# A written-out head for an attention and density kernel: statistics, weights, projections and maxima ahead of the loop

## The chip, the cores and the metric

The kernel runs on one core of one Trainium2 chip. The metric is the device time of one execution in microseconds. The profile is one execution on the same chip, with the start and end of every instruction.

## The reference, cut to what matters

The input is x of 8 images, 192 channels, 64 x 64 pixels (N = 4096 pixels per image), in fp32. Layer 0 is an attention over the pixels of an image with a residual, layer 1 a density model per channel with a residual.

```python
# layer 0: gn is a group norm over 32 groups of 6 channels
q = prelu(conv1x1(gn(x), w1, b1), a1)            # 24 channels
k = prelu(conv1x1(gn(x), w2, b2), a2)            # 24 channels
v = prelu(conv1x1(gn(x), wa, ba), aa)            # 192 channels
score = softmax(einsum('bnc,bcm->bnm', q, k), axis=2)
x = x + einsum('bnm,bmc->bnc', score, v)
# layer 1: per channel a chain 1 -> 3 -> 3 -> 3 -> 1, at gn(x) - 0.5 and gn(x) + 0.5
logits = einsum('cij,cjn->cin', softplus(ms[i]), logits) + bs[i]
logits = logits + tanh(fs[i]) * tanh(logits)      # after the first three layers
x = x + maximum(abs(sigmoid(sign * upper) - sigmoid(sign * lower)), 1e-6)
```

## The kernel before

A tile holds 64 groups of three channels twice: partitions 0 to 63 are the first half of the pixels, 64 to 127 the second half. Eight pieces `d` of an image (`NP`), each 256 pixels of both halves, are the unit of the projections; two loads of 192 KB bring one. Pieces of image 0 wait in the buffers `d3` to `d10` of the density's pool (`xi["first", 0, d]`).

**The loop** (from L1258) runs over 8 x 128 = 1024 steps `t`. A step has the score products of step t + 1 (`scores`, L701, with an exponential on ScalarE, L705), the products and the reduce of a row maximum `LEAD` = 22 steps ahead (`max_step`, L644 and L648), and the attention product of step t (`attend`, L716: 16 matmul instructions). The projections, statistics and maxima of the next image, and the density of the image before, are put between the steps by a planner. It keeps a table of due times (`at`, `due`) and a list of jobs (`job`, `start_job`) that need room in PSUM: of the two accumulators `turns` (b0, b1) the one that attention does not use in these 16 steps is the guests' place (`misc`), and `guest` says from when each of its two banks is free. A job has a rank and the number of banks that it takes. What is written in the program's order stays in that order on each engine: there is no other scheduler. PSUM holds four pairs of banks: b0, b1, `sc` and `mx`.

**The head** is what stands before the loop, and it is where the change is. In order of the program:

- 16 loads of image 0 on SP's queue (L103).
- `ident`, and on VectorE `gavg`, the matrix that averages over groups.
- On ScalarE's queue the slopes (L152), eight loads of biases (L170, L171, which wait for VectorE's memsets of `bq` and the reduce into `bk`), eight loads of weights (L181 to L184) and 22 small loads of the density's parameters (L215).
- VectorE copies the weights into the layout of the matmuls (L187 to L198) and works out the density's parameters (L230 to L274: softplus of `mm`, products of the first two linear layers, and so on), with one Exp and one Tanh on ScalarE (L231, L246).
- Statistics of image 0 (`norm_stat`, L378: 16 instructions), aggregation and the group's mean and variance over TensorE (`norm_end`, L387 to L426), weights times the scale (`weights`, L469 to L501).
- `settle` runs the planner until it has nothing to do: `keys` of all eight pieces and `queries` of the first two (L544, L573), each followed by two ScalarE evacuations with Relu (L529) into one of two scratch pairs `pra`, `prb`, and one VectorE instruction that makes PReLU of them (L532).
- `values` (L601), two jobs per piece, are handed to the planner, and 22 calls of `max_step` follow, one planner step each. All projections go through the same guests' place, all maxima through `mx`. When sixteen maxima are there, `max_end` transposes them (L668) and adds them to q (L673).

A maximum of one chunk covers 128 rows of scores and 1024 columns: two matmuls that contract over 24 rows, each in a row group of 32, then one reduce. Chunk `k` uses the row groups 0 and 1 where `k` is even, 2 and 3 where it is odd.

Of the kernel before, what the change touches and what calls it, by code (L numbers as in the profile page):

```python
# [9 lines left out]
F32 = mybir.dt.float32  # L10
AF = mybir.ActivationFunctionType
# [6 lines left out]
def kernel(  # L18
# [131 lines left out]
    slope = const.tile([128, 3], F32, name="slope")  # L150
    for i, a in enumerate((a1, a2, aa)):
        nc.scalar.dma_start(out=slope[:, i : i + 1], in_=a.partition_broadcast(128))  # L152
    nslope = const.tile([128, 3], F32, name="nslope")
    nc.vector.tensor_scalar(nslope, slope, -1.0, None, ALU.mult)

# [7 lines left out]
    for t in (w1r, w2r, bq, ba_row, one_row):  # L163
        nc.vector.memset(t, 0.0)
# [4 lines left out]
    for k in range(4):  # L169
        nc.scalar.dma_start(out=bq[32 * k : 32 * k + CR, 0:1], in_=b1.unsqueeze(1))  # L170
        nc.scalar.dma_start(out=bk[32 * k : 32 * k + CR, 0:1], in_=b2.unsqueeze(1))  # L171
    for t in (bq, bk):
        nc.vector.tensor_scalar(t[:, 1:2], t[:, 0:1], -1.0, None, ALU.mult)
# [11 lines left out]
    for k in range(4):  # L185
        at = slice(32 * k, 32 * k + CR)
        nc.vector.tensor_copy(w1r[:, :, at], s1)  # L187

        p = slice(R * (k % 2), R * (k % 2) + R)
        nc.vector.tensor_copy(w2r[p, :, at], s2[p])  # L190
    for g in range(3):
        nc.vector.tensor_copy(
            wa_sb[:, g, :].rearrange("p (h r) -> p h r", h=3),
            sa[:, g, :].rearrange("p (r h) -> p h r", h=3),
        )
    for s in range(2):
        p = slice(R * s, R * s + 1)
        nc.vector.tensor_copy(  # L198
            ba_row[p].rearrange("p (h r) -> p h r", h=3),
            sb[p].rearrange("p (r h) -> p h r", h=3),  # L200
        )
# [7 lines left out]
    for src, dst, at, n in (  # L209
# [4 lines left out]
        for s in range(2):  # L214
            nc.scalar.dma_start(  # L215
                out=dst[R * s : R * s + R, :, at : at + n],
                in_=src.rearrange("(r g) i j -> r g (i j)", g=3),
            )


# [7 lines left out]
    sp = bufs[1][:, 0:432].rearrange("p (a g n) -> p a g n", a=6, g=3)  # L228
    e = sp[:, 0]
    nc.vector.scalar_tensor_tensor(e, mm, -1.0, mm, ALU.mult, ALU.max)  # L230
    nc.scalar.activation(e, e, AF.Exp, scale=-1.0)  # L231
    d = sp[:, 1]
    nc.vector.tensor_scalar(d, e, 2.0, None, ALU.add)
    nc.vector.reciprocal(d, d)
    s = sp[:, 2]
    nc.vector.tensor_tensor(s, e, d, ALU.mult)
    z = sp[:, 3]
    nc.vector.tensor_tensor(z, s, s, ALU.mult)
    p = sp[:, 4]
    nc.vector.tensor_scalar(p, z, 1.0 / 15.0, None, ALU.mult)  # L240
    for k in (13.0, 11.0, 9.0, 7.0, 5.0, 3.0):
        nc.vector.scalar_tensor_tensor(p, p, 1.0 / k, z, ALU.add, ALU.mult)
    nc.vector.scalar_tensor_tensor(p, p, 1.0, s, ALU.add, ALU.mult)
    nc.vector.tensor_scalar(d, mm, 0.0, None, ALU.max)
    nc.vector.scalar_tensor_tensor(wsp, p, 2.0, d, ALU.mult, ALU.add)
    nc.scalar.activation(tf, ff, AF.Tanh)  # L246
    q = sp[:, 5, :, 0:3]
    nc.vector.tensor_copy(lb, cb[:, :, 3:6])
    for j in range(3):
        w1j = wsp[:, :, 3 + j : 12 : 3]  # L250
        nc.vector.tensor_tensor(
            lc[:, :, j::3], w1j, tf[:, :, j : j + 1].to_broadcast([128, 3, 3]), ALU.mult
        )
        nc.vector.tensor_tensor(
            q, w1j, cb[:, :, j : j + 1].to_broadcast([128, 3, 3]), ALU.mult
        )
        nc.vector.tensor_tensor(lb, lb, q, ALU.add)
        dst = q if j else la
        nc.vector.tensor_tensor(
            dst, w1j, wsp[:, :, j : j + 1].to_broadcast([128, 3, 3]), ALU.mult  # L260
        )
        if j:
            nc.vector.tensor_tensor(la, la, q, ALU.add)

# [3 lines left out]
    nc.vector.tensor_copy(wx[:, :, 0, :], wsp[:, :, 0:3])  # L268
    nc.vector.tensor_copy(wx[:, :, 1, :], la)
    for i, k in enumerate((-0.5, 0.5)):  # L270
        nc.vector.scalar_tensor_tensor(
            bx[:, i, :, 0, :], wsp[:, :, 0:3], k, cb[:, :, 0:3], ALU.mult, ALU.add
        )
        nc.vector.scalar_tensor_tensor(bx[:, i, :, 1, :], la, k, lb, ALU.mult, ALU.add)  # L274
# [12 lines left out]
    guest = [0, 0]  # L287
# [10 lines left out]
    def misc():  # L298
        return turns[(now[0] // STEPS + 1) % 2]
# [10 lines left out]
    def start_job(t):  # L310
        p = t % STEPS
        for n, (rank, make, hold, banks, cols) in enumerate(jobs):
            if stream[0] and (p < 3 or p + max(hold, 1) >= STEPS):
                continue
            at_ = [i for i in range(2) if guest[i] <= t]
            if len(at_) < banks:
                if rank < 2:
                    return
                continue
# [4 lines left out]
            pm = misc()  # L324
# [302 lines left out]
    def max_step(m):  # L627
        b, n, i = m // IMG, m % IMG // STEPS, m % STEPS
        if b >= B:
            return  # L630
        if i == 0:
            rowmax[b, n] = small.tile([128, 4, 4], F32, tag="rm", bufs=3, name=f"rm_{b}_{n}")
# [18 lines left out]
        if i == STEPS - 1:  # L651
            max_end(b, n)
# [662 lines left out]
```

## Time and profile before

| what | us |
|---|---|
| median of 3 runs | 5038.0 (5033.52 to 5038.48) |
| the profiled execution, its own time | 5034.38 |
| its span, first to last instruction | 5032.6 |
| TensorE busy in the span | 4804.2 (95%) |
| VectorE busy | 4306.7 (86%) |
| ScalarE busy | 3204.3 (64%) |
| GpSimd busy | 510.7 (10%) |
| first attention product starts at | 167.10 |

The profile's lines name a kernel line (L716), the engine, the operation and its tiles (written <- read). A number behind x is a count of instructions; an fp32 matmul makes two in the records. In brackets stands the idle time before and what ended it. PE is TensorE, PEld its weight loads, DVE VectorE, ACT ScalarE, POOL GpSimd; SPq and ACTq are the queues on which these engines issue DMAs. PEclk is the share of its full clock that TensorE was granted. Times count from the first instruction. Idle time of an engine that others don't wait for costs nothing.

### The profile page before, as it was taken

The numbers are of one execution on the slowest core, as the hardware profiler recorded it, in microseconds if no ns is written. First come the engines' busy times: TensorE is split into PE (matmuls) and PEld (weight loads), VectorE is DVE, ScalarE is ACT, GpSimd is POOL, SyncE is SP. The second block draws the span as 40 slices with busy tenths as digits, with TensorE's granted clock in tenths as the row PEclk, the third lists the DMA queues.
The fourth block names the chain that finished last, engine by engine and source line by source line (L and its number), as shares of the span: only waits on it lengthen the run. The fifth ranks groups of instructions, "written<-read, shape, count | busy, mean of one in ns | idle before, by whom it ended". The sixth has DMA issues, their size and how long they took to land.

```text
span 5032.6 us, 69853 instructions
## 1 busy us (share of the span) xinstructions
PE 4804.2 (95%) x29152; PEld 3531.2 (70%) x29152; DVE 4306.7 (86%) x4455; ACT 3204.3 (64%) x3710; POOL 510.7 (10%) x493
## 2 busy tenths in 40 slices
PE   4999999999999999999999999999999999999596
PEld 2677777777777777777777777777777777777342
DVE  3433338999899998999899998999899998999878
ACT  1233336777677766777677766677677776677765
POOL 0000000111111200120101110120111110120000
PEclk9999999999999999999999999999999999999798
DMA  2000011010111112001111112001110111000000
GB/s 54 26 16 10 20 28 30 21 37 24 35 30 30 28 34 46 18 22 39 33 33 28 27 34 49 18 18 41 37 33 22 33 27 25 11 10 17 9 9 17
DMA packets 111952, 135.48 MB, mean 27 GB/s; under 512 B 14738, under 2 KB 93076, under 8 KB 111636
## 3 DMA queue, kind: packets, MB, share of 16 engines
q1 hardware_dynamic: 105856, 130.58, 10.6%
q8 instruction: 228, 3.74, 0.3%
q10 hardware_dynamic: 5780, 0.44, 0.1%
q14 instruction: 88, 0.72, 0.1%
HBM read 105.82 MB, written 25.17 MB: 26 GB/s over the span
## 4 chain that ended last, share of the span: by engine, by line
PE 72%; DVE 23%; ACT 3%; issue 1%; DMA 1%; POOL 1%; ACTq 0%; POOLq 0%; DVEq 0%
PE b L716 42%; PE sc L701 16%; DVE d L958 15%; DVE rm L648 5%; PE b L601 3%; PE b L899 2%; PE mx L644 2%; PE b L573 2%; PE b L544 1%; PE sc_tail L899 1%; PE mx_tail L899 1%; DVE st L378 1%; PE b L749 1%; ACT d L951 1%; PE b L668 1%
## 5 line engine op out<-in xcount | busy, mean ns | idle before, releaser
L716 PEld LDWEIGHTS b<-v,e 128*128 128x128 f32 x16384 | 2660.0, 190 | 779.1 <-issue 779.1
L716 PE MATMUL b<-v,e 128*128 128x193 f32 x16384 | 2963.8, 335 | 0.0
L705 ACT ACTIVATE e<-sc 128x1024 f32<-128x1024 f32 x1024 | 1046.2, 1022 | 1412.9 <-PE mx L644 1349.0
L648 DVE TENSOR_REDUCE rm<-mx 128x1 f32<-128x1024 f32 x1024 | 1248.8, 1220 | 556.5 <-PE mx L644 552.3
L644 PE MATMUL mx<-k,q 24*128 24x512 f32 x4096 | 1164.5, 645 | 23.4 <-DVE rm L648 23.1
L701 PE MATMUL sc<-q,k 25*128 25x512 f32 x4096 | 1158.1, 642 | 4.2 <-ACT e L705 4.0
L958 DVE SCALAR_TENSOR_TENSOR d<-d,wsp,d 128x1024 f32<-128x1024 f32 x768 | 985.6, 1284 | 47.3 <-ACT d L951 35.2
L958 DVE SCALAR_TENSOR_TENSOR d<-d,lc,d 128x1024 f32<-128x1024 f32 x765 | 968.3, 1279 | 16.3 <-ACT d L935 3.3
L958 DVE SCALAR_TENSOR_TENSOR d<-d,tf,d 128x1024 f32<-128x1024 f32 x543 | 681.4, 1280 | 4.0 <-ACT d L941 3.9
L941 ACT ACTIVATE d<-d 128x1024 f32<-128x1024 f32 x543 | 570.1, 1055 | 72.2 <-DVE d L958 71.3
L701 PEld LDWEIGHTS sc<-q,k 25*128 25x128 f32 x4096 | 307.2, 183 | 237.3 <-issue 201.2
L1040 POOL MEMSET pause<- 128x1 f32 x240 | 23.7, 99 | 4079.3 <-DVE d L958 4079.3
L951 ACT ACTIVATE d<-d,cb,wsp 128x1024 f32<-128x1024 f32 x351 | 433.1, 1235 | 7.1 <-DVE d L958 5.6
L926 ACT ACTIVATE d<-xc,bn,wn 128x1024 f32<-128x1024 f32 x288 | 353.3, 1233 | 4.5 <-DVE bn L438 4.4
L644 PEld LDWEIGHTS mx<-k,q 24*128 24x128 f32 x4096 | 309.1, 184 | 64.5 <-DVE rm L648 60.2
L935 ACT ACTIVATE d<-xc,bn,wn 128x1024 f32<-128x1024 f32 x255 | 314.5, 1234 | 0.1
L1087 POOL TENSOR_TENSOR d<-d,d 128x512 f32<-128x512 f32 x80 | 168.2, 2102 | 0.1
L1075 POOL TENSOR_TENSOR d<-d,d 128x512 f32<-128x512 f32 x80 | 166.3, 2078 | 7.8 <-DVE d L958 7.1
L1095 POOL TENSOR_TENSOR d<-d,d 128x512 f32<-128x512 f32 x80 | 159.6, 1995 | 2.1 <-POOL pause L1040 0.3
L601 PE MATMUL b<-wv,xi 64*128 64x192 f32 x1344 | 139.5, 340 | 0.0
L601 PEld LDWEIGHTS b<-wv,xi 64*128 64x128 f32 x1344 | 106.5, 186 | 25.4 <-issue 23.8
L1079 ACT ACTIVATE d<-d 128x512 f32<-128x512 f32 x160 | 91.8, 623 | 32.9 <-POOL d L1075 26.0
(157 smaller groups left out, 2337.3 us busy)
## 6 DMA issues: line engine op xcount, KB each, us to landing
xi<-in_x_dram SPq DMA_DIRECT2D x392, 192.0 KB, 3.5
xc<-in_x_dram SPq DMA_DIRECT2D x64, 384.0 KB, 5.8
out_dram<-xc SPq DMA_DIRECT2D x96, 256.0 KB, 3.1
d<-in_x_dram SPq DMA_DIRECT2D x16, 192.0 KB, 3.6
d<-in_wat_dram ACTq DMA_DIRECT2D x2, 144.0 KB
cb<-in_den_b_dram ACTq DMA_DIRECT2D x6, 2.2 KB
ff<-in_den_f_dram ACTq DMA_DIRECT2D x6, 2.2 KB, 4.8
bq<-in_b_dram ACTq DMA_DIRECT2D x4, 0.1 KB
```

The lines of the kernel that those rows point to most:

```text
L601: nc.tensor.matmul(pv[:, s, 0:C], lhsT=t[p, g, k * 128 : k * 128 + 128] if g < 3 else one_row[p], rhs=wf["v", b][p, g, :] if g < 3 else wf ...
L644: nc.tensor.matmul(sc[:, s, :], lhsT=tile_of(qt[b, n // 2], n, j)[r], rhs=kt[b][r, u : u + F], start=True, stop=True,)
L648: nc.vector.tensor_reduce(out=rowmax[b, n][:, j, k : k + 1], in_=sc, axis=AX.XY, op=ALU.max)
L701: nc.tensor.matmul(sc[:, s, :], lhsT=kt[b][r, k : k + 128], rhs=qt[b, n // 2][r, :, u : u + 256], start=True, stop=True,)
L705: return lambda: nc.scalar.activation(e, sc, AF.Exp)
L716: nc.tensor.matmul(a[:, j, 0 : C + 1], lhsT=e[:, s, j * 128 : j * 128 + 128], rhs=v[:, s, p % 4, :], start=p == 0 and s == 0 and j % 2 == ...
L899: nc.tensor.matmul(out[:, h, :], lhsT=diag[g][:, 3 * i + n - 1 if n else 9 + i, :], rhs=src[:, h * F : h * F + F], start=n == 0, stop=n == 3,)
L926: nc.scalar.activation(self.buf[k], self.src(), AF.Tanh, bias=bn[:, s, g, 0, i : i + 1], scale=wn[:, g, 0, i : i + 1],)
L935: nc.scalar.activation(self.buf[k], self.src(), AF.Identity, bias=bn[:, s, g, 1, i : i + 1], scale=wn[:, g, 1, i : i + 1],)
L941: nc.scalar.activation(self.buf[k], self.buf["l", k[1], k[2]], AF.Tanh)
L951: nc.scalar.activation(self.buf[k], self.buf["l", n - 1, 0], AF.Identity, bias=offset, scale=wsp[:, g, w : w + 1],)
L958: nc.vector.scalar_tensor_tensor(dst, src, factor, dst, ALU.mult, ALU.add)
```

## The change

The 16 statistics now stand ahead of everything else on VectorE but the first memsets; the copies of the weights go to GpSimd (`spread`), and the sign changes of biases and slopes stand behind the statistics (`negatives`). On ScalarE's queue the weights come first, then biases and slopes; the 22 parameter loads go to SP's queue, behind image 0.

The density's parameters become a generator, `parameters`, with the same 36 VectorE and two ScalarE instructions. The loop takes one of them per step from step 4 on, ahead of the step's scores and maxima.

The planner gets a list of rooms, `homes`, in place of `misc` and `guest`: a job goes to the room that has been free longest. In the head these are b0, b1 and the pairs `sc` and `mx`; in the loop there is one again, the accumulator that attention leaves free.

The head after the weights is written out: each planner step takes the next projection of a list (query 0, key 0, query 1, keys 1 to 7, then the sixteen values in attention's order), and from the ninth step on a pair of maxima, chunks `k` and `k + 1`, one into `sc` and one into `mx`: both products first, then both reduces. Eight such pairs make the sixteen maxima of the first block; key 6 and key 7 stand among the first of them, since chunks 0 and 1 need keys 0 to 3 alone. Six single maxima of the second block follow, each into `sc`. `max_step` is split into `place`, `max_products` and `max_reduce`; in the loop it does what it did. The line numbers of the changed kernel: statistics L407, aggregation L416, scaled weights L498, keys L573, queries L602, values L630, maxima L669 and L677, scores L738, attention L753.

```diff
-    slope = const.tile([128, 3], F32, name="slope")
-    for i, a in enumerate((a1, a2, aa)):
-        nc.scalar.dma_start(out=slope[:, i : i + 1], in_=a.partition_broadcast(128))
-    nslope = const.tile([128, 3], F32, name="nslope")
-    nc.vector.tensor_scalar(nslope, slope, -1.0, None, ALU.mult)
-
...
-    for t in (w1r, w2r, bq, ba_row, one_row):
+    slope = const.tile([128, 3], F32, name="slope")
+    nslope = const.tile([128, 3], F32, name="nslope")
+    for t in (bq, w1r, w2r, ba_row, one_row):
         nc.vector.memset(t, 0.0)
     nc.vector.memset(one_row[0:1], 1.0)
...
-    for k in range(4):
-        nc.scalar.dma_start(out=bq[32 * k : 32 * k + CR, 0:1], in_=b1.unsqueeze(1))
-        nc.scalar.dma_start(out=bk[32 * k : 32 * k + CR, 0:1], in_=b2.unsqueeze(1))
-    for t in (bq, bk):
-        nc.vector.tensor_scalar(t[:, 1:2], t[:, 0:1], -1.0, None, ALU.mult)
...
     for k in range(4):
-        at = slice(32 * k, 32 * k + CR)
-        nc.vector.tensor_copy(w1r[:, :, at], s1)
-
-        p = slice(R * (k % 2), R * (k % 2) + R)
-        nc.vector.tensor_copy(w2r[p, :, at], s2[p])
-    for g in range(3):
-        nc.vector.tensor_copy(
-            wa_sb[:, g, :].rearrange("p (h r) -> p h r", h=3),
-            sa[:, g, :].rearrange("p (r h) -> p h r", h=3),
-        )
-    for s in range(2):
-        p = slice(R * s, R * s + 1)
-        nc.vector.tensor_copy(
-            ba_row[p].rearrange("p (h r) -> p h r", h=3),
-            sb[p].rearrange("p (r h) -> p h r", h=3),
-        )
+        nc.scalar.dma_start(out=bq[32 * k : 32 * k + CR, 0:1], in_=b1.unsqueeze(1))
+        nc.scalar.dma_start(out=bk[32 * k : 32 * k + CR, 0:1], in_=b2.unsqueeze(1))
+    for i, a in enumerate((a1, a2, aa)):
+        nc.scalar.dma_start(out=slope[:, i : i + 1], in_=a.partition_broadcast(128))
+
+    def spread():
+
+        for k in range(4):
+            at = slice(32 * k, 32 * k + CR)
+            nc.gpsimd.tensor_copy(w1r[:, :, at], s1)
+
+            p = slice(R * (k % 2), R * (k % 2) + R)
+            nc.gpsimd.tensor_copy(w2r[p, :, at], s2[p])
+        for g in range(3):
+            nc.gpsimd.tensor_copy(
+                wa_sb[:, g, :].rearrange("p (h r) -> p h r", h=3),
+                sa[:, g, :].rearrange("p (r h) -> p h r", h=3),
+            )
+        for s in range(2):
+            p = slice(R * s, R * s + 1)
+            nc.gpsimd.tensor_copy(
+                ba_row[p].rearrange("p (h r) -> p h r", h=3),
+                sb[p].rearrange("p (r h) -> p h r", h=3),
+            )
+
+    def negatives():
+        for t in (bq, bk):
+            nc.vector.tensor_scalar(t[:, 1:2], t[:, 0:1], -1.0, None, ALU.mult)
+        nc.vector.tensor_scalar(nslope, slope, -1.0, None, ALU.mult)
+
     negmax = const.tile([128, 4, 128], F32, name="negmax")
...
     ):
         for s in range(2):
-            nc.scalar.dma_start(
+            nc.sync.dma_start(
...
-    sp = bufs[1][:, 0:432].rearrange("p (a g n) -> p a g n", a=6, g=3)
-    e = sp[:, 0]
-    nc.vector.scalar_tensor_tensor(e, mm, -1.0, mm, ALU.mult, ALU.max)
-    nc.scalar.activation(e, e, AF.Exp, scale=-1.0)
...
+    def parameters():
+
+
+        sp = bufs[1][:, 0:432].rearrange("p (a g n) -> p a g n", a=6, g=3)
+        e = sp[:, 0]
+        nc.vector.scalar_tensor_tensor(e, mm, -1.0, mm, ALU.mult, ALU.max)
+        yield
+        nc.scalar.activation(e, e, AF.Exp, scale=-1.0)
+        yield
+        d = sp[:, 1]
+        nc.vector.tensor_scalar(d, e, 2.0, None, ALU.add)
+        yield
...
-    guest = [0, 0]
...
-    def misc():
-        return turns[(now[0] // STEPS + 1) % 2]
+
+    homes = []
 
...
-            at_ = [i for i in range(2) if guest[i] <= t]
-            if len(at_) < banks:
+            rooms = [(pm, g) for pm, g in homes if sum(k <= t for k in g) >= banks]
+            if not rooms:
                 if rank < 2:
...
-            pm = misc()
+            pm, guest = min(rooms, key=lambda r: max(r[1]))
+            at_ = [i for i in range(2) if guest[i] <= t]
             for i in at_[:banks]:
...
-    def max_step(m):
-        b, n, i = m // IMG, m % IMG // STEPS, m % STEPS
-        if b >= B:
-            return
-        if i == 0:
-            rowmax[b, n] = small.tile([128, 4, 4], F32, tag="rm", bufs=3, name=f"rm_{b}_{n}")
+    def place(m):
+
 
         p = (m - LEAD + 1) % STEPS
-        odd = p < STEPS // 2
         j, k = divmod(p % 8, 2)
-        k = 2 * k + odd
-        assert ("q", b, n) in made and all(("k", b, d) in made for d in range(NP))
-        sc = ps_mx.tile([128, 2, F], F32, tag="mx", name=f"mx_{b}_{n}_{i}")
+        return m // IMG, m % IMG // STEPS, j, 2 * k + (p < STEPS // 2)
+
+    def max_products(b, n, j, k, sc):
+        assert all(i in made for i in (("q", b, n), ("k", b, 2 * k), ("k", b, 2 * k + 1)))
         for s in range(2):
             g = 2 * (k % 2) + s
             r = slice(32 * g, 32 * g + CR)
...
                 sc[:, s, :], lhsT=tile_of(qt[b, n // 2], n, j)[r], rhs=kt[b][r, u : u + F],
                 start=True, stop=True,
             )
+
+    def max_reduce(b, n, j, k, sc):
+        if (b, n) not in rowmax:
+            rowmax[b, n] = small.tile([128, 4, 4], F32, tag="rm", bufs=3, name=f"rm_{b}_{n}")
         nc.vector.tensor_reduce(
             out=rowmax[b, n][:, j, k : k + 1], in_=sc, axis=AX.XY, op=ALU.max
         )
-        if i == STEPS - 1:
+
+    def max_step(m):
+        b, n, j, k = place(m)
+        if b >= B:
+            return
+        sc = ps_mx.tile([128, 2, F], F32, tag="mx", name=f"mx_{m}")
+        max_products(b, n, j, k, sc)
+        max_reduce(b, n, j, k, sc)
+        if m % STEPS == STEPS - 1:
             max_end(b, n)
 
...
+    spread()
+    negatives()
+    others = [
+        ps_sc.tile([128, 2, F], F32, tag="sc", name="sc_head"),
+        ps_mx.tile([128, 2, F], F32, tag="mx", name="mx_head"),
+    ]
+    homes.extend((t, [0, 0]) for t in turns + others)
+
+    def go_on():
+        work_off(now[0], 0.0)
+        now[0] += 1
 
     def settle():
         while jobs or any(k <= now[0] + 8 for k in due):
-            work_off(now[0], 0.0)
-            now[0] += 1
+            go_on()
 
     norm_end((0, 0), 2 * NP, 0, lambda: weights(0, lambda: None))
     settle()
-    for d in range(NP):
-        use(0, d, "first", now[0], 1, d < 2, 0)
-    settle()
-    for d in range(NP):
-        use(0, d, "first", now[0], 0, 0, 1)
-    for m in range(LEAD):
-        max_step(m)
-        work_off(now[0], 0.0)
-        now[0] += 1
+
+    todo = [(queries, 0), (keys, 0), (queries, 1)] + [(keys, d) for d in range(1, NP)]
+    todo += [(values, 2 * c + h, k) for c in ORDER for h in range(2) for k in range(2)]
+    ahead = deque([] for _ in range(8))
+    for k in (0, 2):
+        ahead.extend([(0, j, k), (0, j, k + 1)] for j in range(4))
+        ahead.append([])
+    ahead.extend([place(m)[1:]] for m in range(STEPS, LEAD))
+    while todo or ahead:
+        if todo:
+            make, d, *k = todo.pop(0)
+            make(0, d, *k, "first", lambda: None)
+        pair = list(zip(others, ahead.popleft() if ahead else ()))
+        if pair and len(homes) > 2:
+            del homes[2:]
+        for t, (n, j, k) in pair:
+            max_products(0, n, j, k, t)
+        for t, (n, j, k) in pair:
+            max_reduce(0, n, j, k, t)
+        if (0, 3, 3) in [i for _, i in pair]:
+            max_end(0, 0)
+        go_on()
     settle()
     assert not due and not loads
     now[0] = 0
-    guest[:] = 0, 0
     ready[:] = 0, 0
+    rest = parameters()
     stream[0] = True
 
...
         now[0] = t
+        if t % STEPS == 0:
+            homes[:] = [(turns[(t // STEPS + 1) % 2], [0, 0])]
+        if 3 < t < IMG:
+            next(rest, None)
+        assert t != IMG or next(rest, 0) == 0
         run = scores(t + 1) if t + 1 < last else None
...
+    homes[:] = [(turns[1], [0, 0])]
```

More of the change, by code (lines that the diff above doesn't have):

```diff
@@ L227 @@
     lc = const.tile([128, 3, 9], F32, name="lc")
-    sp = bufs[1][:, 0:432].rearrange("p (a g n) -> p a g n", a=6, g=3)
-    e = sp[:, 0]
-    nc.vector.scalar_tensor_tensor(e, mm, -1.0, mm, ALU.mult, ALU.max)
-    nc.scalar.activation(e, e, AF.Exp, scale=-1.0)
[L232 to L263, printed above, removed]
@@ L266 @@
     wx = const.tile([128, 3, 2, 3], F32, name="wx")
     bx = const.tile([128, 2, 3, 2, 3], F32, name="bx")
[L268 to L274, printed above, removed]
+    def parameters():
[8 more added lines that the diff above has]
+        yield
+        nc.vector.reciprocal(d, d)
+        yield
+        s = sp[:, 2]
+        nc.vector.tensor_tensor(s, e, d, ALU.mult)
+        yield
+        z = sp[:, 3]
+        nc.vector.tensor_tensor(z, s, s, ALU.mult)
+        yield
+        p = sp[:, 4]
+        nc.vector.tensor_scalar(p, z, 1.0 / 15.0, None, ALU.mult)
+        yield
+        for k in (13.0, 11.0, 9.0, 7.0, 5.0, 3.0):
+            nc.vector.scalar_tensor_tensor(p, p, 1.0 / k, z, ALU.add, ALU.mult)
+            yield
+        nc.vector.scalar_tensor_tensor(p, p, 1.0, s, ALU.add, ALU.mult)
+        yield
+        nc.vector.tensor_scalar(d, mm, 0.0, None, ALU.max)
+        yield
+        nc.vector.scalar_tensor_tensor(wsp, p, 2.0, d, ALU.mult, ALU.add)
+        yield
+        nc.scalar.activation(tf, ff, AF.Tanh)
+        yield
+        q = sp[:, 5, :, 0:3]
+        nc.vector.tensor_copy(lb, cb[:, :, 3:6])
+        yield
+        for j in range(3):
+            w1j = wsp[:, :, 3 + j : 12 : 3]
+            nc.vector.tensor_tensor(
+                lc[:, :, j::3], w1j, tf[:, :, j : j + 1].to_broadcast([128, 3, 3]), ALU.mult
+            )
+            yield
+            nc.vector.tensor_tensor(
+                q, w1j, cb[:, :, j : j + 1].to_broadcast([128, 3, 3]), ALU.mult
+            )
+            yield
+            nc.vector.tensor_tensor(lb, lb, q, ALU.add)
+            yield
+            dst = q if j else la
+            nc.vector.tensor_tensor(
+                dst, w1j, wsp[:, :, j : j + 1].to_broadcast([128, 3, 3]), ALU.mult
+            )
+            yield
+            if j:
+                nc.vector.tensor_tensor(la, la, q, ALU.add)
+                yield
+        nc.vector.tensor_copy(wx[:, :, 0, :], wsp[:, :, 0:3])
+        yield
+        nc.vector.tensor_copy(wx[:, :, 1, :], la)
+        yield
+        for i, k in enumerate((-0.5, 0.5)):
+            nc.vector.scalar_tensor_tensor(
+                bx[:, i, :, 0, :], wsp[:, :, 0:3], k, cb[:, :, 0:3], ALU.mult, ALU.add
+            )
+            yield
+            nc.vector.scalar_tensor_tensor(bx[:, i, :, 1, :], la, k, lb, ALU.mult, ALU.add)
+            yield
```

## The prediction

> **What bounds the kernel now.** I read the page first, then busy time by stage, then the chain of waits of the first 62 us, the waits and the timeline of the stage behind it.
>
> ```profile
> span 5032.6 us, 69853 instructions
> ```
>
> The columns of the next view are: stretch, its length, busy time (and instructions) of TensorE, its weight loads, VectorE, ScalarE and GpSimd, granted clock, DMA share, GB/s.
>
> ```profile
> core 0: us, PE busy (x) PEld busy (x) DVE busy (x) ACT busy (x) POOL busy (x), PEclk, DMA share, GB/s
> 30.00:51.37 21.37, 0.00 (x1) 0.00 (x1) 13.93 (x52) 3.05 (x4) 0.00 (x0) 1.00 0.49 100
> 51.37:61.63 10.26, 6.20 (x22) 5.48 (x23) 2.65 (x17) 1.99 (x4) 0.00 (x0) 1.00 0.00 0
> 61.63:88.00 26.37, 18.11 (x80) 12.18 (x82) 5.34 (x10) 9.18 (x20) 0.00 (x0) 1.00 0.00 1
> 88.00:161.30 73.30, 62.15 (x330) 36.08 (x328) 35.35 (x40) 12.20 (x28) 0.00 (x0) 0.74 0.00 0
> 167.10:4690.00 4522.90, 4474.96 (x28170) 3372.55 (x28166) 3959.47 (x4044) 2957.11 (x3421) 509.34 (x480) 0.99 0.11 28
> ```
>
> The loop (167 to 4690) is TensorE's: busy 99%. Everything before 167.10, where the first attention product starts, is a head in which no engine is full. The order of instructions of the two programs is the same on every engine behind the head, but for 36 VectorE and 2 ScalarE instructions (the density's parameters) put into the first 40 of 1024 steps. So the question is how much earlier the loop starts, and what those 38 cost in it. The chain of waits shows what the start waits for:
>
> ```profile
> 15.24 3.54 DMA d<-in_w2t_dram
> 18.79 3.50 DMA d<-in_x_dram
> ...
> 30.71 3.46 DMA ff<-in_den_f_dram
> 34.19 5.87 DMA xc<-in_x_dram
> ...
> 43.32 7.38 DVE st L378 x16
> 50.73 0.60 DVE mv L387
> ```
>
> The last piece of image 0 lands at 22.29 (18.79 + 3.50), yet its statistics start at 43.24: VectorE is in order, and ahead of them stand the weights' copies and 36 parameter instructions, which wait for 22 small loads (ScalarE's queue, 0.62 to 0.84 us per issue) up to about 38.9.
>
> Then one bank at a time:
>
> ```profile
> 77.60 1.56 PE L544 MATMUL b<-d,wk 128*128 128x256 f32 x6 [0.92 <-ACT prb L529]
> 79.20 0.83 ACT L529 ACTIVATE pra<-b,bk 64x256 f32<-64x256 f32 x2 [1.65 <-PE b L544]
> 80.09 1.56 PE L544 MATMUL b<-d,wk 128*128 128x256 f32 x6 [0.92 <-ACT pra L529]
> ```
>
> A key projection comes every 2.49 us because the next waits for ScalarE to empty the same bank. In the stage behind it, maxima and values, the waits alternate between TensorE and VectorE over one bank pair (mx), and the clock falls to 0.74:
>
> ```profile
> DVE rm L648 <- PE mx L644: 39.2, 22, 3.6
> ...
> PE mx L644 <- DVE rm L648: 10.0, 8, 1.3
> ```
>
> ```profile
> 90.37 1.25 PE L601 MATMUL b<-wv,d 64*128 64x192 f32 x12
> ...
> 94.33 1.13 PE L644 MATMUL mx<-k,q 24*128 24x512 f32 x4 [1.33 <-DVE rm L648]
> ...
> 95.38 2.29 PE L601 MATMUL b<-wv,d 64*128 64x192 f32 x12
> ```
>
> The same value projection takes 1.25 us at full clock and 2.29 at half.
>
> **The change, step by step.**
>
> *Statistics first.* The copies (13 VectorE instructions) go to GpSimd, the parameters into the loop, the 22 loads to the end of SP's queue behind the 16 pieces of image 0. ScalarE's queue now starts with the eight weight loads and no longer waits for VectorE's late memsets; it and SP's queue still issue the same 35 loads ahead of the statistics, at 140 to 180 GB/s in either program, so I leave the last piece at about 22.3. A pair of statistics follows each piece (7.38/16 = 0.46 each), so two are left: 23.2. Three sign changes (0.15 to 0.17 each, issued 0.2 apart) stand before the aggregation and wait for the biases and slopes, last on ScalarE's queue; I take 23.8 for the aggregation instead of 50.73: **26.9 us**. If the slopes land 2 us later, or the pieces 2 us earlier, it is 25 to 29.
> GpSimd's copies must be done when the weights are scaled (L469), 4.3 us behind the aggregation, so at about 28. No copy of its kind is in the trace: its memset of 512 took 0.52 us and its two-input operation of 512 took 2.0 to 2.1, so 8 copies of 72 and 5 of 192 cost 1.8 to 6.4 us; I take 5, nearer to the second row, since these read too. The weights come first on their queue; from about 12 they are done by 18. Ten us of cover hide them; without it they would cost those 5.
> From aggregation to first projection nothing changes (51.37 to 61.63 less the 0.6 before): the first projection starts at 61.6 - 26.9 = **34.7**.
>
> *Projections over four bank pairs.* The first query, [...]took 2.93; a key takes 1.28 when it follows at once (71.34: two in 2.86, less the tail), a query 1.46. In the new order eight groups run before the first maxima: 2.9 + 1.4 + 1.46 + 5 x 1.28 = 12.1 us. ScalarE needs 0.84 per key and 1.28 per query, VectorE 0.48 and 0.75: both stay under TensorE. First pair at 46.8.
>
> *Maxima in pairs.* Eight pairs replace sixteen single steps; between them stand the last two keys and seven values. VectorE: two reduces at 1.14 apart (95.50 to 96.64) and one PReLU at 0.53: 2.8 us. TensorE: the two chunks of a pair use different row groups. The loop shows such products side by side:
>
> ```profile
> 171.56 0.70 PE L701 MATMUL sc<-q,k 25*128 25x512 f32 x2
> 171.58 0.70 PE L644 MATMUL mx<-k,q 24*128 24x512 f32 x2
> ```
>
> So a pair with a value costs 1.06 + 1.50 = 2.6, or 3.6 if the second product starts only when the first is done. VectorE frees the second bank 1.1 us behind the first, so the two mostly overlap in part; following the order with these durations I get 3.4 a pair: 8 x 3.4 = 27.2 (before: 50 us for the same sixteen). 74.0.
>
> *The rest.* One bank of transposes 0.66, six single maxima at 1.06, nine values at 1.50, now bound by TensorE: 20.5. 94.5. From the last value to the first attention product as before, 162.65 to 167.10 (a table load of 1.28 and the first exponential in it): 4.5. 99.0.
>
> *The clock.* The records show that it fell in the stretch of 3.4 us behind one with little full-width work (less than about 0.8 of a value projection; the maxima, on 24 rows, seem to count for nearly nothing) and that key projections of one per 2.5 us kept it up. Before, the same durations at full clock sum to 91 of the 105.5 us between 61.63 and 167.1: 14 lost. [...] By the trace, the pairs carry at most one value per 3.4 us, near the edge: two to four stretches at half clock, each worth 3.4 x (1 - 1/1.9) = 1.6, so 3 to 6, and some 3 that this way of following the order also missed before. I add 7 and go by the trace: the first attention product at **106**, against 167.1: **61 us earlier**.
>
> *Parameters in the loop.* 36 VectorE instructions (7.2 us in all before), one per step, each ahead of that step's maximum. From 180 to 660 VectorE was busy 178.82 of 480 us, so 2.4 us a step are free; a 0.2 us instruction in front of a 1.22 us reduce delays the bank's return by 0.2 where TensorE comes back for it only after 2.81 us of attention. Nothing. The two ScalarE ones (0.26, 0.23) fit in its free half and need no table load: before, one load served Exp and Tanh. If that cover were gone, all 38 cost 7.7. The loads for image 1, queued on SP behind 22 issues of 0.65 (14 us), are first used some 20 us into the loop; they would be issued by 35 to 46.
>
> The sum: the profiled execution took 5034.38 (span 5032.6): 4973. The three runs shown have a median of 5038.0, 3.6 above; against that it is 4977. I say 4976.
>
> **The rivals.**
> 1. *Half clock through the head* (12%). Pairs with waits keep the array under the edge, as at 88 to 161. At half clock from end to end the stage from 34.7 would be 108 us, and the gain 24; with ten stretches instead of three, 11 us more than mine: gain 45 to 50, 4990. For it: 0.74 before. Against: fewer idle gaps, more values per stretch.
> 2. *Statistics late* (4%). Slopes or pieces land late, or GpSimd's copies take three times my figure: projections at 45 instead of 34.7, 4987. Against: the same loads in the same 20 us.
> 3. *Slower: the loop loses its clock in image 0* (2%). A parameter instruction that waits for ScalarE's Exp or Tanh holds VectorE and the maximum behind it; TensorE misses the bank, and an attention stretch goes to half clock. It decides where a wait exceeds the 1.4 us or so of slack between a reduce's end and the next use of its bank: at 1.6 us per half stretch it takes 38 such steps to undo 61 us, and only two instructions wait for ScalarE. If the low clock held through the 127 steps of image 0, 490 us would become about 700: 5185.
> 4. *Side by side in name only* (within my case). Products one after the other: 3.6 a pair, +2 to 4 us.
>
> **How the numbers follow.** Forecast 80%, its own range a gain of 52 to 68 (4970 to 4986); rivals as above; 2% for no gain left by a cause that I do not see. Range 4967 to 4990: the early ends of the loads and a full clock give 68 to 70 us, rival 1 begins at 48. About 0.2% (10 us) is what a measurement here tells from no change. Faster 0.96, same 0.01, slower 0.03.
>
> **What would show it.** Right: the aggregation (L416) near 24, the first query near 35, reduces in twos, the first L753 product near 106, the loop's step still 3.88 us, the end earlier by the same 61. Wrong: ScalarE's scaling (L498) waiting for GpSimd, a clock under 0.75 between 35 and 106, or TensorE waiting on VectorE between 106 and 260.

## The result and the profile after

The changed kernel takes 4970.7 us (median of 4 runs, 4970.10 to 4971.12), the kernel before 5038.2 in the same rounds: a ratio of 0.9866, 95% interval 0.9849 to 0.9883. The profiled execution took 4970.59, its span is 4968.6: 64.0 us less than before. Timed once more on another occasion it took 4968.3 (4963.74 to 4969.47) against 5036.8: ratio 0.9863, interval 0.9848 to 0.9877.

From the page after:

```profile
span 4968.6 us, 69863 instructions
```

Busy time by stage, after. The stages end at the aggregation, the first query, the first pair of maxima, the transposes, the first attention product and the last:

```profile
core 0: us, PE busy (x) PEld busy (x) DVE busy (x) ACT busy (x) POOL busy (x), PEclk, DMA share, GB/s
0.00:23.25 23.25, 0.00 (x0) 0.00 (x0) 11.05 (x35) 1.28 (x1) 5.07 (x26) 1.00 0.69 153
23.25:32.42 9.17, 5.36 (x22) 5.16 (x23) 2.45 (x15) 1.99 (x4) 0.00 (x0) 1.00 0.16 4
32.42:45.83 13.41, 13.41 (x63) 10.47 (x62) 4.21 (x11) 6.68 (x14) 0.00 (x0) 1.00 0.95 198
45.83:72.84 27.01, 25.94 (x189) 15.17 (x189) 23.54 (x28) 7.96 (x19) 0.00 (x0) 1.00 0.10 20
72.84:97.43 24.59, 22.31 (x185) 14.34 (x185) 13.95 (x18) 10.68 (x22) 0.00 (x0) 1.00 0.00 1
97.43:4620.00 4522.57, 4478.83 (x28164) 3376.55 (x28160) 3957.09 (x4075) 2953.45 (x3418) 508.82 (x480) 0.99 0.11 28
```

Before, TensorE was idle for most of the first 62 us, waited between the projections up to 88 and then ran at a clock of 0.74. Now it is busy from 32 on, and behind its first projections the clock is 1.00 up to 97.43. In the stage of the pairs (45.83 to 72.84) TensorE is busy 25.94 and VectorE 23.54 of 27.01 us: both engines are close to full.

The chain of waits, after, its beginning:

```profile
14.37 5.33 DMA d<-in_x_dram
...
22.61 0.54 DVE st L407
23.34 0.50 DVE mv L416
...
27.57 0.62 ACT wq L498
...
33.25 2.56 PE sc_head L602 x11
35.81 1.92 PE mx_head L573 x6
37.73 1.50 PE b L602 x12
```

Before, 28 us lay between the landing of the last piece of image 0 (22.29) and the aggregation (50.73): VectorE took its instructions in the program's order, the last parameter at 43.16 and the first statistic at 43.24. Now one statistic of 0.54 and three sign changes lie there. The first projections follow one another in `sc_head`, `mx_head` and `b`, without an evacuation between them.

GpSimd's groups of instructions up to 30 us, after (count, busy time, mean ns of one, idle time before):

```profile
L191 POOL COPY wa_sb<-d 128x192 f32<-128x192 f32 x3 | 1.2, 427 | 0.1
L189 POOL COPY w2r<-d 64x72 f32<-64x72 f32 x4 | 1.0, 240 | 0.1
L186 POOL COPY w1r<-d 128x72 f32<-128x72 f32 x4 | 1.0, 240 | 5.5 <-DMA d<-in_w2t_dram 5.4
L197 POOL COPY ba_row<-d 1x192 f32<-1x192 f32 x2 | 0.9, 426 | 0.1
```

The 13 copies take 4.1 us. By the timeline the last ends at 11.4, 16 us before the weights are scaled at 27.57 (L498).

The timeline, after, of one pair of maxima with a value behind it:

```profile
59.41 0.70 PE L669 MATMUL sc_head<-k,q 24*128 24x512 f32 x2
...
59.42 0.70 PE L669 MATMUL mx_head<-k,q 24*128 24x512 f32 x2
...
60.48 1.25 PE L630 MATMUL b<-wv,d 64*128 64x192 f32 x12
60.59 1.23 DVE L677 TENSOR_REDUCE rm<-sc_head 128x1 f32<-128x1024 f32 x1 [1.02 <-PE mx_head L669]
...
61.73 1.22 DVE L677 TENSOR_REDUCE rm<-mx_head 128x1 f32<-128x1024 f32 x1
```

Here the two chunks' products start within 0.01 us of each other, and the value fills TensorE while VectorE reduces both. That is so in two of the eight pairs. In the other six the second product starts 0.22 to 1.02 us behind the first, in four of them because its bank still waits for VectorE's reduce. Before, VectorE waited for the product ahead of every one of its 22 reduces (39.2 us in all).

### The profile page after: what moved, and what is told of

The parts are those of the page before. It is cut to its first block, busy times and chain, and to the rows that moved or that the text cites. A ratio compares the mean times of both kernels' runs of the same rounds, so it can differ in the third digit from the quotient of the medians.

```text
span 4968.6 us, 69863 instructions
## 1 busy us (share of the span) xinstructions
PE 4785.8 (96%) x29152; PEld 3525.8 (71%) x29152; DVE 4301.2 (87%) x4442; ACT 3202.4 (64%) x3709; POOL 513.9 (10%) x506
## 3 DMA queue, kind: packets, MB, share of 16 engines
q1 hardware_dynamic: 110432, 130.65, 10.9%
## 4 chain that ended last, share of the span: by engine, by line
PE 73%; DVE 22%; ACT 3%; issue 1%; POOL 1%; DMA 0%; POOLq 0%; ACTq 0%; SPq 0%; DVEq 0%
PE b L753 43%; PE sc L738 17%; DVE d L995 14%; DVE rm L677 5%; PE b L630 3%; PE b L936 2%; PE b L602 1%; PE b L573 1%; PE mx L669 1%; PE sc_tail L936 1%; PE mx_tail L936 1%; PE b L786 1%; ACT d L988 1%; ACT d L963 1%; PE b L705 1%
## 5 line engine op out<-in xcount | busy, mean ns | idle before, releaser
L753 PEld LDWEIGHTS b<-v,e 128*128 128x128 f32 x16384 | 2668.4, 191 | 781.5 <-issue 781.5
L753 PE MATMUL b<-v,e 128*128 128x193 f32 x16384 | 2972.7, 335 | 0.0
L677 DVE TENSOR_REDUCE rm<-mx 128x1 f32<-128x1024 f32 x1002 | 1222.0, 1220 | 522.2 <-PE mx L669 518.5
L738 PE MATMUL sc<-q,k 25*128 25x512 f32 x4096 | 1159.7, 642 | 5.5 <-ACT e L742 5.2
L669 PE MATMUL mx<-k,q 24*128 24x512 f32 x4008 | 1135.6, 643 | 13.1 <-DVE rm L677 13.0
L978 ACT ACTIVATE d<-d 128x1024 f32<-128x1024 f32 x543 | 570.1, 1055 | 70.8 <-DVE d L995 69.3
L738 PEld LDWEIGHTS sc<-q,k 25*128 25x128 f32 x4096 | 306.8, 183 | 238.6 <-issue 198.8
L669 PEld LDWEIGHTS mx<-k,q 24*128 24x128 f32 x4008 | 300.2, 183 | 40.1 <-DVE rm L677 39.9
L630 PE MATMUL b<-wv,xi 64*128 64x192 f32 x1344 | 139.5, 340 | 0.0
L630 PEld LDWEIGHTS b<-wv,xi 64*128 64x128 f32 x1344 | 106.5, 186 | 25.4 <-issue 23.8
```

The source lines that it names most:

```text
L630: nc.tensor.matmul(pv[:, s, 0:C], lhsT=t[p, g, k * 128 : k * 128 + 128] if g < 3 else one_row[p], rhs=wf["v", b][p, g, :] if g < 3 else wf ...
L669: nc.tensor.matmul(sc[:, s, :], lhsT=tile_of(qt[b, n // 2], n, j)[r], rhs=kt[b][r, u : u + F], start=True, stop=True,)
L677: nc.vector.tensor_reduce(out=rowmax[b, n][:, j, k : k + 1], in_=sc, axis=AX.XY, op=ALU.max)
L738: nc.tensor.matmul(sc[:, s, :], lhsT=kt[b][r, k : k + 128], rhs=qt[b, n // 2][r, :, u : u + 256], start=True, stop=True,)
L753: nc.tensor.matmul(a[:, j, 0 : C + 1], lhsT=e[:, s, j * 128 : j * 128 + 128], rhs=v[:, s, p % 4, :], start=p == 0 and s == 0 and j % 2 == ...
L978: nc.scalar.activation(self.buf[k], self.buf["l", k[1], k[2]], AF.Tanh)
```

## The experiments

Two theories stood after the result. The first: the head's gain is the sum of two independent parts (statistics early, and the order written out over four rooms), and most of the second part is the clock, which before was 0.74 from 88 to 161. The second: the parts need each other, or the pairs gain by row groups alone. A second question was open: the head ended 69.7 us earlier and the span is only 64.0 shorter. Did the loop lose the difference through the parameters put into it, or through something else?

**e1_statistics_only**: the kernel before, with only the prologue changed.

```diff
 # on the kernel before: weights first, copies on GpSimd, parameters as a generator
+    spread()
+    negatives()
...
+        if 3 < t < IMG:
+            next(rest, None)
```

> The kernel before with the first half of the change alone: statistics and weights first, copies on GpSimd, parameter loads on SP's queue, parameters in the loop; projections and maxima of the head as they were, through the planner. Theory (the head's parts add up): aggregation near 23 instead of 50.7, the first query near 34, the loop's first attention product 26 to 29 us earlier than before, about 139 to 141 (half-clock stretches may fall otherwise and move it by 5). Rival (the loop pays for the parameters): the step times of image 0 grow, by up to 7.7 us in all. Total 5006 to 5016.

Measured: 5010.1 (5009.03 to 5011.65), ratio 0.9947 (0.9930 to 0.9964). The aggregation stands at 23.66 (27.1 us earlier), the first attention product at 142.72 (24.4 earlier). The difference was lost right behind the weights. Timeline of this kernel, its first projections:

```profile
34.62 2.93 PE L602 MATMUL b<-d,wq 64*128 64x256 f32 x12 [0.95 <-DVE ba L530]
...
38.92 2.93 PE L573 MATMUL b<-d,wk 128*128 128x256 f32 x6 [1.36 <-ACT pra L558]
...
42.76 2.93 PE L602 MATMUL b<-d,wq 64*128 64x256 f32 x12 [0.92 <-ACT prb L558]
...
47.06 4.27 PE L573 MATMUL b<-d,wk 128*128 128x256 f32 x12 [1.37 <-ACT pra L558]
```

In the trace before, the second of these (L544) took 1.56 us. There only the first query took 2.93 us; here three projections did, and the two keys at 47.06 took 4.27 us together, before 2.86: some 4 us more, of which less time at half clock later in the head wins back about 1.4. The gaps are not what differs, since before they were the same (1.36, 0.92). What differs is when the trace's clock records begin, both with full clock: here at 49.97, 15.35 us behind the start of the first query, before at 64.68, 3.05 us behind it. So part of the 27 us was lost again in slow first projections. Why they stayed slow for longer here was not shown.

**e2_written_out_only**: the changed kernel with the old prologue.

```diff
 # on the changed kernel: prologue of before, parameters ahead of everything again
-    spread()
-    negatives()
...
-        if 3 < t < IMG:
-            next(rest, None)
```

> The changed kernel with the first half undone: statistics behind the parameters, as before; four places for projections and maxima in pairs remain. Theory: aggregation near 50.7, and from the first query to the first attention product about 65 us instead of 105.5, so the loop starts near 125, 41 us earlier than before. Total 4997 less what the clock takes in the loop: if the 6.5 us that the changed kernel gives back behind step 150 come from the place of the loop in the clock's stretches of 3.4 us, this kernel gives back another amount, 0 to 8 us; the rival, that parameters or their loads in the loop cause it, has this one give back nothing, since both are in the head here.

Measured: 4996.4 (4994.08 to 4997.70), ratio 0.9919 (0.9904 to 0.9933). The first attention product stands at 124.47, 42.6 us earlier than before, and behind the slow first projections no stretch of the head is at half clock (the clock is 1.00 from 60 to 116). The two parts alone give 24.4 + 42.6 = 67.0 of the 69.7 us that they give together. They are nearly independent; the missing 2.7 us are as much as e1 lost in its first projections (4.1 less 1.4). The theory's other half, that most of the second part is the clock, did not hold: a clock of 0.74 over the 73.3 us from 88.00 to 161.30 before means 38 us at half clock. As a value takes 2.93 us at half clock in that trace and 1.57 at full, that costs some 18 us (an estimate), under half of the 42.6.

**e3_parameters_before_loop**: the 38 parameter instructions all made just ahead of the loop.

```diff
     rest = parameters()
+    for _ in rest:
+        pass
```

> The changed kernel with all 38 parameter instructions issued in one go ahead of the loop, behind the last values. Theory (the slots in the loop are free, and here the cover is mostly gone): VectorE is busy 7 to 8 us longer from about 94.6; the first maxima of the loop wait for it, and the loop loses 3 to 6 us in its first two steps. Rival (also free, since only maxima 22 steps ahead wait): 0 us. Total 4970.7 plus that, with up to 5 us either way from the clock in the loop.

Measured: 4973.6 (4971.47 to 4974.30), ratio 0.9873 (0.9858 to 0.9888). The first attention product comes 3.9 us later than in the changed kernel (101.29), but 3.0 of these stand ahead of the parameters. The first scores start at 95.95 instead of 92.98: the aggregation is 0.8 us later (24.05), and a stretch at half clock lies at 76.08, where the two programs are still the same and the changed kernel's two profiles have none. From the first scores to the exponential of step 3 it takes 15.49 us, in the changed kernel 14.06: about 1.4 us are what the parameters can have cost in front of the loop, less than the 3 to 6 expected and the 7.7 of their own durations. The medians, 3 to 5 us above those of the changed kernel on other occasions, can't be put down to them. Nor does this kernel's loop decide on the parameters: it is 4.8 us longer than before, but 3.3 of these come ahead of step 100, with a stretch at half clock at 226.27 that the changed kernel doesn't have. That decision comes from the second profile and from e2 (below).

**e4_pairs_same_rows**: the two chunks of a pair on the same row groups.

```diff
-        ahead.extend([(0, j, k), (0, j, k + 1)] for j in range(4))
+        for i in range(2):
+            ahead.extend([(0, j, k + i), (0, j + 1, k + i)] for j in (0, 2))
```

> The changed kernel with pairs made of two row tiles of the same chunk, so both products use the same two row groups and can't run beside each other. Theory (side by side is worth something): the second product starts 1.06 us behind the first in every pair, and the eight pairs take 2 to 4 us longer than the 27 us from the first pair to the transposes. Rival (VectorE frees the second bank later anyway, so the rows hardly matter): at most 1 us. Total 4970.7 plus that, with up to 5 us either way from the clock in the loop.

Measured: 4972.3 (4966.68 to 4976.31), ratio 0.9870 (0.9856 to 0.9885). In the timeline of this kernel the second product starts 0.96 us behind the first, which takes 1.13:

```profile
60.22 1.13 PE L669 MATMUL sc_head<-k,q 24*128 24x512 f32 x4
...
61.18 1.02 PE L669 MATMUL mx_head<-k,q 24*128 24x512 f32 x4
```

The eight pairs take 29.70 instead of 27.01 us: the different row groups are worth 2.7 us, which the totals do not show.

**e5_one_bank_pair**: the same order, but every maximum of the head in one bank pair.

```diff
-            max_products(0, n, j, k, t)
-        for t, (n, j, k) in pair:
-            max_reduce(0, n, j, k, t)
+            max_products(0, n, j, k, others[0])
+            max_reduce(0, n, j, k, others[0])
```

> The changed kernel with all maxima of the head in one bank pair, product and reduce in turn, the order of the projections unchanged. Theory (the second bank pair carries the gain of the maxima's stage): a pair takes two turns of product 1.17 and reduce 1.23 plus hand-overs, 4.9 us instead of 3.4; first pair to transposes 38 to 40 us instead of 27, and TensorE waits more, so half-clock stretches come back and add 3 to 10. First attention product 109 to 120. Rival (the order of the projections carries it): under 4 us later.

Measured: 4997.6 (4994.25 to 5001.01), ratio 0.9923 (0.9908 to 0.9938): 27 us above the changed kernel. The first attention product comes at 125.16, later than the 109 to 120 expected. Busy time of its sixteen maxima, and two waits of this kernel between 45 and 100 us (total, times, longest):

```profile
45.36:99.95 54.59, 43.97 (x189) 23.77 (x189) 24.92 (x28) 7.72 (x18) 0.00 (x0) 0.72 0.04 8
```

```profile
DVE rm L677 <- PE sc_head L669: 30.4, 16, 3.0
...
PE sc_head L669 <- DVE rm L677: 10.6, 8, 1.3
```

The same 189 TensorE instructions as in the changed kernel's stage take twice as long. TensorE idles only 10.6 us, never over 1.3 at a time, but the clock falls to 0.72, and then VectorE waits for slower products. Of the 42.6 us that the written-out head gives, 27.6 hang on this second bank pair (54.59 against 27.01). They can be split: 9.6 us are more idle time of TensorE (10.62 against 1.07), 2.7 are the side by side that e4 measures, and some 14 are the clock (an estimate: 0.72 means 30.6 of the 54.59 us at half clock, and a value takes 2.93 there, 1.57 at full).

What half clock comes behind can be read from the traces. In those of the kernels before and after, all changes of the clock lie whole multiples of 3.41 us apart (after: 98.09, 101.50, 726.14, 729.55, 780.75 and so on), on a grid. Here are stretches of this grid with the value products alone (L601 and L630; columns: TensorE, its weight loads, clock, DMA share, GB/s), of the kernel before, of this one and of the changed one:

```profile
102.22:105.64 3.42, 1.07 (x12) 1.07 (x14) 1.00 0.00 0
105.64:109.05 3.41, 1.47 (x12) 0.97 (x10) 0.50 0.02 5
```

```profile
76.34:79.75 3.41, 1.57 (x16) 1.28 (x16) 1.00 0.00 0
79.75:83.16 3.41, 0.43 (x5) 0.44 (x7) 1.00 0.02 5
83.16:86.58 3.42, 2.11 (x14) 1.60 (x12) 0.50 0.00 0
```

```profile
60.55:63.96 3.41, 1.50 (x16) 1.21 (x16) 1.00 0.02 5
63.96:67.37 3.41, 2.10 (x22) 1.80 (x24) 1.00 0.00 0
```

Between the last key and the first attention product the twelve traces of this study hold 22 whole stretches at full clock with 1.08 us of values or less. Half clock follows 21 of them; the one exception, 0.99 us in the changed kernel at 70.78, has four transposes beside it. It follows no stretch with 1.20 or more. At half clock the divide lies between 2.33 and 2.36 us. A pair of the changed kernel takes 3.38 us (27.01 by 8), so nearly every stretch holds one value; here a pair takes 6.8, and stretches come without one. This is a regularity of twelve traces; no run sets the values of a stretch alone.

**d1_delay_1us and d2_delay_2us**: the changed kernel with one or two memsets on VectorE ahead of the aggregation, to move the whole head against this grid.

```diff
     negatives()
+    for _ in range(1):  # range(2) in d2
+        nc.vector.memset(bufs[16], 0.0)
```

> The changed kernel with one memset of 128 x 1024 on VectorE ahead of the aggregation of image 0: about 1 us more on the chain, nothing else. Theory (the 6.5 us given back in the loop depend on where the loop lies in the clock's stretches): the loop starts about 1 us later, but the total differs from 4970.7 + 1 by some us, since the half-clock stretches of the loop (17 of 3.4 us) fall elsewhere. Rival (they come from the work in the loop): total 4971.7 within 1 us, stretches at the same steps.

> The same with two memsets, about 2 us more on the chain. Theory: a total unlike 4970.7 + 2, with another number of half-clock stretches in the loop than 17. Rival: 4972.7 within 1 us.

Measured: d1 4970.2 (4965.10 to 4975.27), ratio 0.9872 (0.9855 to 0.9888); d2 4968.3 (4965.94 to 4970.51), ratio 0.9865 (0.9850 to 0.9879). As a dial the delays failed: one program's runs already differ by 10 us. But the traces answered the question in another way, together with the next two runs.

**e8_scores_early**: the scores and the exponential of step 0 ahead of the last two value projections (two, where the expectation says three).

```diff
+    begun = []
...
+        if not ahead and len(todo) == 2 and ("max", 0, 0) in made:
+            begun.append(scores(0))
+            begun[0]()
...
-    scores(0)()
+    if not begun:
+        scores(0)()
```

> The changed kernel with the scores and the exponential of step 0 issued ahead of the last three values, so that the table load of 1.28 us and the first exponential run beside their projections. Theory: the 4.45 us from the last value to the first attention product shrink by 2 to 3.5, and the loop starts near 94 to 95.5. Total 4967 to 4969, with up to 5 us either way from the clock in the loop. Rival (ScalarE, busy with the values' evacuations, is in order, and the exponential delays these): nothing gained.

Measured: 4964.4 (4963.65 to 4965.24), ratio 0.9857 (0.9842 to 0.9872). That is 6.3 us below the changed kernel, but on another occasion. So both were run again in the same rounds.

> The changed kernel itself, timed on the same chip and in the same rounds as the kernel with the early scores. Both theories of the remaining gain need its spread: that the runs of one kernel differ by up to 10 us (4965 to 4975, as those with the delay of 1 us did) by where the half-clock stretches fall in the loop, expects a median of 4967 to 4973 and a distance between the lowest and the highest run of 5 us or more; that its time is fixed by the program expects 4970 to 4971.5 in every run, as in its first four.

> The scores of step 0 ahead of the last two value projections, again, beside the changed kernel on the same chip. The head's wait for the table load and the first exponential is shorter by 2.6 us (the first attention product at 94.9 instead of 97.4): a median 2 to 3 us below the changed kernel's if that is all, 6 us below if the first comparison's distance (4964.4 against 4970.7, measured on different occasions) is the edit's own, and no distance that can be told if the loop's half-clock stretches differ by more from run to run.

Measured: the changed kernel 4968.3 (4963.74 to 4969.47), with the early scores 4965.8 (4961.96 to 4969.64). The ranges overlap; a gain in the total can't be told from these runs. In the traces it is plain and the same twice: from the transposes to the first attention product 22.89 and 22.90 us with the early scores, 24.59 and 24.66 without. The timelines show why, first the changed kernel's, then that with the early scores:

```profile
93.99 1.28 ACT L742 ACT_TABLE_LOAD   x1
...
96.36 0.70 PE L738 MATMUL sc<-q,k 25*128 25x512 f32 x2 [2.25 <-ACT e L742]
```

```profile
86.69 1.28 ACT L742 ACT_TABLE_LOAD   x1
...
90.92 1.25 PE L630 MATMUL b<-wv,d 64*128 64x192 f32 x12 [0.39 <-ACT pra L558]
```

TensorE's wait of 2.25 us for the table load and the first exponential becomes one of 0.39. The early scores do more than that. With TensorE's wait the half-clock stretch goes that lies on the first attention product in both profiles of the changed kernel (98.09 and 96.22): from the transposes to the second attention product it takes 26.74 and 26.75 us, without the early scores 30.15 and 30.10. So this version is the best of the study by its head, by 3.4 us, which is still under what a run's total varies by.

**Where the loop's 6.5 us went.** The exponential of a step (first column: start) in three traces, against the trace before:

| step | before | after | earlier by | after, second profile | earlier by |
|---|---|---|---|---|---|
| 0 | 164.95 | 95.28 | 69.7 | 94.21 | 70.7 |
| 100 | 593.36 | 523.71 | 69.6 | 522.59 | 70.8 |
| 165 | 875.60 | 809.27 | 66.3 | 804.84 | 70.8 |
| 290 | 1434.89 | 1371.97 | 62.9 | 1364.05 | 70.8 |
| 1023 | 4676.16 | 4613.01 | 63.1 | 4605.26 | 70.9 |

Through the first hundred steps, with all 38 parameter instructions in them, nothing is lost. The loss comes between steps 100 and 290 in the first profile, and not at all in the second of the same program. Busy time of the same steps, first in the first profile, then in the second:

```profile
780.80:787.60 6.80, 6.80 (x24) 5.26 (x24) 5.00 (x9) 2.15 (x2) 0.00 (x0) 0.50 0.00 1
```

```profile
779.60:786.40 6.80, 6.80 (x44) 5.00 (x44) 6.56 (x11) 3.17 (x3) 0.00 (x0) 1.00 0.00 1
```

At half clock 24 TensorE instructions pass in 6.8 us, at full clock 44. The stretches at half clock are whole multiples of 3.41 us (17 of them, 58.0 us, in the loop of the first profile; 12, 41.0 us, before). Where their grid lies against the loop differs from run to run. Measured from the start of the exponential of step 3, modulo 3.41 us, with the time from that exponential to the one of step 1023:

| trace | grid's place, us | at half clock in the loop, us | step 3 to 1023, us |
|---|---|---|---|
| e5 | 0.12 | 54.6 | 4505.77 |
| d2 | 0.22 | 54.6 | 4504.83 |
| early scores, first | 0.24 | 47.8 | 4502.49 |
| e1 | 0.36 | 41.0 | 4499.27 |
| after, second profile | 0.54 | 41.0 | 4499.34 |
| before | 0.64 | 41.0 | 4499.48 |
| d1 | 0.66 | 41.0 | 4499.47 |
| early scores, second | 0.72 | 47.8 | 4502.83 |
| e2 | 1.00 | 47.8 | 4503.21 |
| e4 | 1.15 | 47.8 | 4503.26 |
| after, first profile | 1.30 | 58.0 | 4505.98 |
| e3 | 2.19 | 47.8 | 4504.26 |

Four different programs, with the parameters in the loop or without, agree within 0.2 us where the grid lies between 0.36 and 0.66. One program, at 0.54 and 1.30, differs by 6.6. The place doesn't account for everything: 0.22 and 0.24 stand beside 54.6 and 47.8 us. But e2, with no parameter in its loop, loses 3.7 us at 1.00, and the changed kernel's second profile, with all of them in it, loses none. So by these traces the loop lost nothing to the change itself: the first profile had the grid at another place than the profile before (1.30, 0.64) and 58.0 us at half clock instead of 41.0. That the place itself decides, and nothing that goes with it, is read from these twelve traces and was not forced: the delays of d1 and d2 did not set it, as one program alone has it at 0.54 and at 1.30.

## Why the prediction was right

The forecast was 4976, the result 4970.7 and 4968.3; the profile's span is 64.0 us shorter (70.9 in the second profile) against a forecast of 61. By its steps:

- **Statistics first**: forecast for the aggregation 23.8, measured 23.25; the gain of 26.9 was 27.5. GpSimd's copies took 4.1 us (taken: 5) and were hidden; the scaling at L498 waits for VectorE, not for GpSimd.
- **First query**: forecast 34.7, measured 32.42. The step "from aggregation to first projection nothing changes" failed. 1.7 of the 2.3 us are here (9.17 from aggregation to query, forecast 10.9), the rest came with the earlier aggregation. The query now has a room of its own, `sc_head`, and no longer waits until VectorE has read the offsets out of the common one (in e1, with the common room, it takes 10.96 from the aggregation; in e2, with its own, 9.12).
- **Eight groups**: forecast 12.1, measured 13.41. The slow start reached into the second group, a key that took 1.99 instead of 1.28, and the first query took 3.3 instead of 2.9. In the second profile the eight groups took 12.72.
- **Pairs**: forecast 27.2, measured 27.01. Followed by hand from durations of the trace before, this was the largest term, and it held: neither all side by side (2.6 a pair) nor one after the other (3.6), but 3.38. "Before: 50 us for the same sixteen" was a misreading: from the first product (86.55) to the transposes (140.52) it was 53.97. e5 shows what the term rested on.
- **The rest**: from the transposes to the end of the last value 20.1 (forecast 20.5), then 4.45 to the first attention product (forecast 4.5).
- **The clock**: this term was mis-sized. "I add 7" for two to four stretches at half clock and an unexplained remainder; there was none ahead of 97.43 in the first profile, and one, at the very end, in the second (96.22). The sum without the term, 99.0, stands against 97.43 and 96.43 measured. What failed is not the criterion ("less than about 0.8 of a value projection" in a stretch): at 1.57 us a value, the divide between 1.08 and 1.20 is at 0.69 to 0.76 of one, at half clock at 0.80. What failed is its use: a pair takes 3.38 us, so a stretch of 3.41 holds one whole value, and in the first profile none from 53.72 to the transposes has less than 1.50 us. Around the transposes the edge is near: there the changed kernel has 0.99 and kept its clock, e3 has 0.72 and lost it. That the maxima count for little was so too: from 91.99 to 95.40 before, TensorE has 0.02 us of values beside 2.08 of maxima, and half clock follows.
- **Parameters in the loop**: forecast nothing, measured 69.7 us of lead at step 0 and 69.6 at step 100.
- **The loop**: "the same" was right for the program. The first profile gave back 6.5 us with 17 us more at half clock than the profile before, which happened to offset most of the mis-sized clock term: that the total came out 5 us from the forecast is in part luck. The second gave back nothing and has 70.9 us. The sign of being wrong that was named for the loop, TensorE waiting on VectorE, did not come: neither profile shows TensorE waiting between 98 and 260.

Short waits alone did not keep the clock in these traces: e5 falls to 0.72 with TensorE's waits at most 1.3 us, and the kernel before to 0.74 from 88 to 161 with waits no longer. The changed kernel has 1.00 up to 97.43. What goes with the difference is how much value work falls in a stretch of 3.41 us (e5 above).

Rival 1 (half clock through the head) is what e5 became, one bank pair away from the change. Rival 4 (side by side in name only) was priced at 2 to 4 us; e4 measured 2.7.

## What to carry to other kernels

In a head where two engines pass one bank pair back and forth, a second pair can be worth far more than the wait it removes: here 27.6 us, of which only 9.6 were more waiting of TensorE, and the clock of the stage was 0.72 with one pair and 1.00 with two. Work that holds up the start (38 small instructions ahead of the statistics) cost nothing, one per step, inside a loop bound by another engine: the lead was 69.7 us at step 0 and 69.6 at step 100. Before explaining a loss of a few microseconds in a long loop, profile the same program twice: here a loss of 6.5 us was gone in the second profile.

## What was not expected of the hardware

- The clock's changes lie on a grid of 3.41 us that does not start with the program: the stretch at half clock on the first attention product starts at 98.09 us in the first profile after and at 96.22 in the second, 1.87 us apart, which is no multiple of 3.41. Against the loop the two have the grid 0.8 us apart, and the loop took 4505.98 and 4499.34 us. Stretches far into the loop lie on it too (3647.95 in the first profile), and the 6.6 us between the two are 0.1% of the span.
- The clock column does not show the slow first projections. In e1 three of them took 2.93 us each, nearly twice the 1.56 of the same key before, in a stretch where the column says 1.00:

```profile
34.62:47.06 12.44, 8.79 (x30) 5.55 (x31) 1.25 (x3) 3.36 (x6) 0.00 (x0) 1.00 1.10 224
```

The trace has no clock record ahead of 49.97, and where there is none the column shows 1.00. The transfers in this stretch (DMA share 1.10) are not the cause: the changed kernel's key at 39.16 took 1.56 us beside a share of 0.95. Until the first record, durations of a known instruction are the surer sign.
